# A causal attention layer in a hand-written order: follow-up pieces at set distances, the maximum subtracted on GpSimd, scores scheduled from the end

## The chip, the cores and the metric

The kernel runs on one core of one Trainium2 chip. A core has five engines that run side by side, each through its own instructions in a fixed order: TensorE (PE in the profile; its weight loads are PEld), VectorE (DVE), ScalarE (ACT), GpSimd (POOL) and SyncE (SP). Engines wait for one another through semaphores. The metric is the device time of one execution in microseconds (us); for a kernel with several runs it is their median.

## The reference

The input is an image of 256 channels and 64 x 64 pixels. Layer 0 is windowed linear attention over the image; the change does not touch it. Layer 1, which the change rewrites in part, treats the pixels as N = 4096 tokens of D = 256 numbers:

```python
t = t + attention(layer_norm(t))          # one head, causal, 4096 x 4096 scores
    A   = where(causal, q @ k.T, -32767) / 16;  out = softmax(A) @ v + x
    out = layer_norm(out) * g + b;  h = relu(out @ W1 + b1) @ W2 + b2
    result = layer_norm(h) * g + b
t = t + experts(layer_norm(t))
    logits = mean over all tokens of x @ Wr + br;  rw = softmax(logits)
    loads  = rw * 4096;  scale = where(loads > 640, 640 / loads, 1)
    rw = softmax(rw * scale);  the best two of 8 experts, for all tokens the same
    two-layer gelu networks of these two, weighted, and a layer_norm
```

The masked scores are filled with a finite number, so that the mask's own exponentials are also added up (`rest` and `after` below). All arithmetic is float32.

## The kernel before, in words

The whole kernel is one program of three stages. Layer 0 runs until about 978 us of the profile, the causal layer from there to about 1665 us, the router (which picks the two experts) to about 1681 us, and the experts to the end at 1908.8 us.

**The causal layer** works on 16 units `h`, each of 256 queries (two tiles of 128 tokens), and on key blocks `b` of 256 keys; unit `h` meets the blocks `h, h-1, ..., 0`. That makes 136 pairs `(h, b)`, in the order of the list `PAIRS`, where long and short units alternate. For each pair there are these steps:

- `scores(h, b)`: 4 matmuls on PE (8 records in the profile, since a float32 matmul shows as two) into the PSUM tile `pa`, L1051. ACT copies the scores to SBUF, `s<-pa`, L1063. DVE then updates a running elementwise maximum `max<-max,pa`, L1067. After the last block of a unit, DVE folds its two halves, L1070. The diagonal block goes through GpSimd for its mask, L1054 to L1060.
- `maxima(h)`: two pieces per unit. `over_keys` transposes the folded maximum on PE, L1080, and DVE reduces it, L1082 and L1086. `turn` transposes it back, L1093, and ACT copies it out as `tops`, L1095.
- `exponentials(h, b)`: DVE subtracts `tops` from the scores, L1102, and ACT takes the exponential, L1103. For the diagonal block the same is done for `rest`, L1106 and L1107.
- `products(h, b, j)`: for each of the two tiles `j`, 2 matmuls of the exponentials with the values into `po`, L1124 (and one of `rest`, L1127, on the diagonal). GpSimd normalises the residual `xn`, L1116, in a tile of which there is one.
- `finish(h, j)`: DVE divides by the softmax's sum and adds the residual, L1137 to L1139, then takes the statistics of the row.

When four tiles (a group `g`) are done, `layers(g, ...)` gives a list of 14 pieces that finish layer 1 for them: `root` (ACT's square root, which needs another activation table than the exponential: a table load of 1.28 us each way), `first` (DVE normalises, GpSimd adds a bias to `t`, L1172), `turn` (PE transposes, L1179; ACT copies, L1180), `hidden` twice (PE L1188, ACT L1190), `last` for each tile (PE L1197, DVE L1199), `root`, `scale` for each tile (DVE, L1207 and L1208), `root`, `norm` (DVE, L1216) and `turn_again` (PE transposes, L1224; ACT copies to `x2` and adds up each row, L1225).

**What sets the order.** PE, DVE and ACT run the instructions in the order in which the program issues them (`manual_schedule`); GpSimd's order is the scheduler's. The main loop runs over the 136 pairs: `score()` issues the scores of the pair that is 19 ahead (the ring of score tiles `s` has 20), `one()` issues one waiting piece, `raise_to(at + 2)` issues the exponentials up to two pairs ahead, then both `products`, then `one()` again. `one()` takes the oldest piece of the list `soon` (maxima, queries, mask fills), and if there is none the oldest of `later` (the layers' pieces). A piece is issued as soon as its turn comes, whether what it needs is ready or not; an engine that meets such an instruction waits. The last unit is walked tile by tile, `j = 1` and then `j = 0`, with all its exponentials issued before.

**The router**, `experts`, begins with the sum of `x2` over all tokens (L1334 to L1339), then a chain of small DVE and ACT operations that ends with the numbers of the two experts, four indirect DMAs from GpSimd's queue that fetch their weights (L1381), and small matmuls for the biases (L1394 to L1404). The experts' matmuls are L1418 and L1438.

Of the kernel before, what the change touches and what calls it, by code (L numbers as in the profile page):

```python
# [11 lines left out]
F32 = mybir.dt.float32  # L12
# [746 lines left out]
RING = 20  # L759
AHEAD = RING - 1  # L760


# [152 lines left out]
class Given:  # L915
# [3 lines left out]
    def __init__(self, nc, a, pool, causal):  # L919
# [21 lines left out]
        self.stats = tile("stats2", [P, NT, 2])  # L941
        self.sums = tile("sums2", [P, DC, NQ + 2])
        self.parts = 0


def causal_attention(tc, t, ident, eps5, causal, big, given):
# [7 lines left out]
    with ExitStack() as ctx:  # L954
# [33 lines left out]
        def behind():  # L988

            sums = sm.tile([NT, D + 1], F32, name="behind", bufs=1)  # L990
            later = sm.tile([NT, NT], F32, name="laters", bufs=1)
# [23 lines left out]
        def fills(h):  # L1015
# [22 lines left out]

            soon.append(turn)

# [58 lines left out]
        def exponentials(h, b):  # L1099
            u = units[h]  # L1100
            s = u[b].rearrange("p (k q) -> p k q", q=2 * P)
            nc.vector.tensor_tensor(s, s, u["top"].unsqueeze(1).to_broadcast([P, 2, 2 * P]), op=ALU.subtract)  # L1102
            nc.scalar.activation(u[b], u[b], AF.Exp, scale=1.0 / 16.0)  # L1103
            if b == h:
                rest = u["rest"].rearrange("p j q -> p (j q)")
                nc.vector.tensor_sub(rest, rest, u["top"][0:NT])  # L1106
                nc.scalar.activation(rest, rest, AF.Exp, scale=1.0 / 16.0)  # L1107
# [23 lines left out]
        def finish(h, j, acc):  # L1131
            i, g, xn = 2 * h + j, h // 2, units[h]["xn"]
            if g not in atts:
                atts[g] = (sm.tile([P, 4, D], F32, name="att"), sm.tile([P, 4, 2], F32, name="mvs", bufs=3), [])
            att, mvs, done = atts[g]
            l = sm.tile([P, 1], F32, name="l")
            nc.vector.reciprocal(l, acc[:, 0:1])  # L1137
            aj = att[:, i - 4 * g, :]
            nc.vector.scalar_tensor_tensor(aj, acc[:, 1:], l, xn[:, j, :], op0=ALU.mult, op1=ALU.add)  # L1139
            statistics(nc, sm, aj, mvs[:, i - 4 * g, :])  # L1140
            done.append(i)
            if 4 * g != BIG:
                if len(done) == 4:
                    later.extend(layers(g, 0, 4))
            elif len(done) == 2:
                later.extend(layers(g, 2, 4))
            elif len(done) > 2:
                new = layers(g, 4 - len(done), 5 - len(done))
                old = later[:]
                later.clear()  # L1150
                while new or old:
                    later.extend(new[:1] + old[:1])
                    del new[:1], old[:1]

        def layers(g, j0, j1):

            att, mvs, _ = atts[g]
            js, width = range(j0, j1), (j1 - j0) * P
            state = {}
# [53 lines left out]
            def norm():  # L1213
                inverse(mine)
                for j in js:
                    nc.vector.tensor_scalar(att[:, j, :].rearrange("p (c q) -> p c q", c=DC),  # L1216
                                            t[:, 4 * g + j, :].rearrange("p (q c) -> p c q", c=DC),
                                            mine[:, j, 0:1], mine[:, j, 1:2], op0=ALU.subtract, op1=ALU.mult)

            def turn_again():  # L1220
                for c in range(DC):
                    pt = psum()
                    for j in js:
                        nc.tensor.transpose(pt[:, (j - j0) * P : (j - j0 + 1) * P], att[:, j, c * P : (c + 1) * P], ident)  # L1224
                    nc.scalar.activation(x2[g][c][:, j0 * P : j1 * P], pt[:, 0:width], AF.Identity,  # L1225
                                         accum_out=given.sums[:, c, given.parts : given.parts + 1])
                given.parts += 1

            return ([lambda: root(mvs), first, turn] + [lambda e=e: hidden(e) for e in range(DC)]
                    + [lambda j=j: last(j) for j in js] + [lambda: root(state["mvy"])]  # L1230
                    + [lambda j=j: scale(j) for j in js] + [lambda: root(mine), norm, turn_again])

        soon, later = [], []

        def one():
            if soon:
                soon.pop(0)()
            elif later:
                later.pop(0)()

        E = mybir.EngineType
        with tc.manual_schedule(engines={E.PE, E.DVE, E.Activation}):
            blocks = [(h, b) for h in PAIRS for b in reversed(range(h + 1))]
            scored, raised = [0], [0]

            def queried(g):
                if g not in qTs:
                    soon.extend(queries(g))

            def score():  # L1250

                at = scored[0]
                if at == len(blocks):
                    return
                scored[0] += 1
                h, b = blocks[at]
                if b == h:
                    while "rest" not in units[h] or not qTs[h // 2][1]:
                        soon.pop(0)()
                    n = PAIRS.index(h) + 1  # L1260
                    if n < len(PAIRS):
                        fills(PAIRS[n])
                        queried(PAIRS[n] // 2)
                scores(h, b)
                if b == 0:
                    soon.extend([lambda: None] + maxima(h))

            def raise_to(at):
                while raised[0] < min(at + 1, len(blocks)):
                    h, b = blocks[raised[0]]  # L1270
                    while "top" not in units[h]:
                        soon.pop(0)()
                    exponentials(h, b)
                    raised[0] += 1
# [4 lines left out]
            causal.values(7, psum)  # L1279
            soon.extend(behind())  # L1280
            fills(PAIRS[0])
            for at in range(AHEAD):
                score()
                one()
                if at in (0, 6):
                    causal.values(6 - at // 6, psum)
                if at == PAIRS[0] + 1:
                    causal.values(4, psum)
            raise_to(1)
            done = [len(blocks) - 1 - PAIRS[-1]]  # L1290
            for at, (h, b) in enumerate(blocks[: done[0]]):
                score()
                one()
                raise_to(at + 2)
                for j in range(2):
                    products(h, b, j)
                one()
            h = PAIRS[-1]
            raise_to(len(blocks))
            for j in (1, 0):  # L1300
                for b in reversed(range(h + 1)):
                    products(h, b, j)
                    for _ in range(2 - j):
                        one()
            while soon or later:
                one()
        return x2


def experts(tc, a, t, out, ident, eps5, given, x2):  # L1310
# [4 lines left out]
    with ExitStack() as ctx:  # L1315
# [16 lines left out]

        xsum = w.tile([P, DC], F32, name="xsum")
        nc.vector.tensor_reduce(xsum, given.sums, AX.X, ALU.add)  # L1334
        every = w.tile([P, DC, P], F32, name="every")
        nc.vector.tensor_copy(every, xsum.unsqueeze(2).to_broadcast([P, DC, P]))
        pl = ps.tile([P, 512], F32, name="pr", bufs=1)
        for c in range(DC):
            nc.tensor.matmul(pl[:, 0:NE], lhsT=every[:, c, :], rhs=given.wr[:, c, :], start=(c == 0), stop=(c == DC - 1))  # L1339
        x = cols("rx")  # L1340
# [3 lines left out]
        sc = cols("sc")  # L1344
        nc.vector.tensor_scalar(sc, rw, float(N), 1.0, op0=ALU.mult, op1=ALU.max)
        nc.vector.reciprocal(sc, sc)
        nc.vector.tensor_scalar(sc, sc, CAPACITY, 1.0, op0=ALU.mult, op1=ALU.min)
        nc.vector.tensor_mul(sc, sc, rw)
        rw = softmax(sc, "sb")
# [15 lines left out]
        hot = w.tile([P, 3, NE], F32, name="hot")  # L1365
        tmp = cols("tmp")
        w1 = w.tile([P, 2, DC * FF], F32, name="w1")
        w2 = w.tile([P, 2, FC * D], F32, name="w2")
        views = [(w1, a["W1e"].rearrange("(r c) f -> r (c f)", c=DC)), (w2, a["W2e"].rearrange("(r c) d -> r (c d)", c=FC))]
        ixs = []  # L1370
        for e in range(2):
            nc.vector.tensor_scalar(hot[:, e, :], rank, float(e), None, op0=ALU.is_equal)
            nc.vector.tensor_mul(tmp, hot[:, e, :], given.ei)
            at = cols(f"at{e}", 1)
            nc.vector.tensor_reduce(at, tmp, AX.X, ALU.add)
            ix = w.tile([P, 1], I32, name=f"ix{e}")
            nc.vector.scalar_tensor_tensor(ix, at, float(P), given.pi, op0=ALU.mult, op1=ALU.add)
            ixs.append(ix)
        for dst, src in views:
            for e in range(2):  # L1380
                nc.gpsimd.indirect_dma_start(  # L1381
                    out=dst[:, e, :], out_offset=None, in_=src,
                    in_offset=bass.IndirectOffsetOnAxis(ap=ixs[e][:, 0:1], axis=0),
                )
        two = cols("two", 2)
        for e in range(2):
            nc.vector.tensor_mul(tmp, hot[:, e, :], rw)
            nc.vector.tensor_reduce(two[:, e : e + 1], tmp, AX.X, ALU.add)
        tw = softmax(two, "sc2")
# [94 lines left out]
```

## Time and profile before

| what | value |
|---|---|
| runs shown | 1910.74, 1914.86, 1917.91 us; median 1914.86 us |
| the profiled execution's own time | 1910.61 us |
| its span, first to last instruction | 1908.8 us |
| mean granted TensorE clock | 0.979 |
| PE / DVE / ACT / POOL busy over the span | 95% / 53% / 43% / 27% |
| causal layer, PE's last product | 978 to 1652.5 us |
| end of layer 1's pieces, first use of their sum by PE | 1666.4 us |
| first experts' matmul, and their unbroken run | 1678.4 us, 1681.6 us |

How to read it: every group of instructions is named by its line, its engine, and the tiles that it writes and reads. "Idle before" is the time in which the engine stood still just before an instruction, and the arrow names what ended that. PE's busy time contains matmuls that run at half the clock, so the granted clock has to be read with it.

### The profile page before, as it was taken

What the parts mean: (1) busy time and instruction counts of PE and PEld (TensorE: products, weight loads), DVE (VectorE), ACT (ScalarE), POOL (GpSimd) and SP (SyncE); (2) the same over time, 40 slices, a digit from 0 to 9 for tenths busy, and PEclk for the clock granted to TensorE, in tenths of its full rate; (3) what the DMA queues carried; (4) which work ended last, traced back from release to release, by engine and by line L of the source; (5) the groups of instructions that cost most, each with busy time, mean ns of one, the idle gap of its engine ahead of it and who ended that gap; (6) DMA issues with size and microseconds to landing.
All of it is one profiled execution on the core that took longest, in us unless ns stands there. A gap on an engine that the chain in (4) does not pass through costs nothing.

```text
span 1908.8 us, 50513 instructions
## 1 busy us (share of the span) xinstructions
PE 1811.1 (95%) x22336; PEld 1323.6 (69%) x22336; DVE 1012.5 (53%) x2019; ACT 828.6 (43%) x1498; POOL 510.0 (27%) x761
## 2 busy tenths in 40 slices
PE   6999999999999999999999999999999888689998
PEld 4666667666666667766678786776777676468777
DVE  7534666655644577667644346445554555533343
ACT  3566444444456644445313335444444434322332
POOL 2493233430254134432120202202112110122120
PEclk9999999999999999999999999999999899789999
DMA  5321100000421100002000000000000000010000
GB/s 177 109 92 63 31 19 16 18 14 20 131 74 36 47 21 18 14 14 53 13 2 1 0 1 1 1 1 1 1 1 1 1 1 1 0 56 11 22 23 22
DMA packets 66651, 53.61 MB, mean 28 GB/s; under 512 B 37312, under 2 KB 56536, under 8 KB 66432
## 3 DMA queue, kind: packets, MB, share of 16 engines
q1 hardware_dynamic: 52688, 27.67, 5.3%
q10 hardware_dynamic: 12480, 18.87, 2.9%
q0 software_dynamic: 1264, 3.84, 0.7%
q8 instruction: 175, 2.87, 0.6%
q14 instruction: 44, 0.36, 0.1%
HBM read 32.93 MB, written 17.44 MB: 26 GB/s over the span
## 4 chain that ended last, share of the span: by engine, by line
PE 42%; DVE 8%; ACT 3%; issue 1%; POOL 0%; ACTq 0%; DVEq 0%
PE pa L1051 10%; PE po L1124 8%; PE ph L1418 6%; PE py L1438 6%; PE pm L1188 2%; PE pm L980 1%; PE pm L1197 1%; DVE max L1067 1%; PE acc L405 1%; DVE lnst L747 1%; PE ps L372 1%; DVE s L1102 1%; ACT s L1063 1%; PE pm L910 1%; PE ps L519 1%
## 5 line engine op out<-in xcount | busy, mean ns | idle before, releaser
L340 ACT ACTIVATE pm<-ps 128x512 f32<-128x512 f32 (+24 forms) x690 | 358.4, 584 | 344.1 <-issue 188.0
L342 DVE TENSOR_SCALAR pm<-ps 128x512 f32<-128x512 f32 (+21 forms) x414 | 265.4, 669 | 264.4 <-PE ps L372 178.2
L372 PE MATMUL ps<-q,kh 32*128 32x217 f32 (+27 forms) x3872 | 212.1, 336 | 0.0
L405 PE MATMUL acc<-pm,vh 128*32 128x217 f32 (+27 forms) x3872 | 199.7, 329 | 0.0
L1051 PE MATMUL pa<-qT,k 128*128 128x256 f32 (+1 forms) x800 | 191.2, 385 | 0.0
L1067 DVE TENSOR_TENSOR max<-max,pa 128x512 f32<-128x512 f32 x105 | 71.8, 684 | 213.7 <-ACT s L1063 213.6
L1051 PEld LDWEIGHTS pa<-qT,k 128*128 128x128 f32 x800 | 153.6, 196 | 24.5 <-issue 3.3
L372 PEld LDWEIGHTS ps<-q,kh 32*128 32x128 f32 x3872 | 160.6, 185 | 9.8
L1103 ACT ACTIVATE s<-s 128x512 f32<-128x512 f32 x136 | 85.5, 630 | 166.7 <-DVE s L1102 166.6
L440 POOL TENSOR_TENSOR y<-y,rn 128x512 f32<-128x512 f32 x32 | 41.0, 1282 | 410.1 <-DVE y L439 410.1
L405 PEld LDWEIGHTS acc<-pm,vh 128*32 128x32 f32 x3872 | 98.0, 109 | 71.8 <-issue 37.1
L363 PE MATMUL ps<-table,table 32*128 32x184 bf16 (+37 forms) x2904 | 141.2, 246 | 5.0 <-ACT pm L340 1.8
L363 PEld LDWEIGHTS <-table 32*128 32x128 bf16 x2904 | 57.6, 92 | 108.0 <-issue 96.1
L1063 ACT COPY s<-pa 128x512 f32<-128x512 f32 x120 | 69.8, 581 | 128.8 <-PE pa L1051 128.5
L1438 PE MATMUL py<-w,hT 128*128 128x256 f32 x512 | 111.8, 379 | 0.0
L1438 PEld LDWEIGHTS py<-w,hT 128*128 128x128 f32 x512 | 97.3, 190 | 15.7 <-issue 1.9
L372 PE MATMUL ps<-q,k 32*128 32x192 f32 (+30 forms) x1936 | 104.1, 338 | 0.5 <-issue 0.5
L1124 PE MATMUL po<-kh,s 128*128 128x257 f32 x406 | 102.6, 385 | 0.9 <-ACT s L1103 0.9
L405 PE MATMUL acc<-pm,v 128*32 128x192 f32 (+30 forms) x1936 | 96.1, 326 | 0.9 <-issue 0.9
L1116 POOL TENSOR_SCALAR xn<-t,stats 128x256 f32<-128x256 f32 x32 | 41.7, 1309 | 205.9 <-DVE att L1139 196.2
L1102 DVE TENSOR_TENSOR s<-s,tops 128x512 f32<-128x512 f32 x136 | 94.3, 698 | 0.0
L519 PE MATMUL ps<-l0wo,y 128*128 128x256 f32 x384 | 90.7, 387 | 0.0
(318 smaller groups left out, 2987.0 us busy)
## 6 DMA issues: line engine op xcount, KB each, us to landing
oscratch<-ov ACTq DMA_DIRECT2D x32, 256.0 KB
ov<-oscratch SPq DMA_DIRECT2D x32, 256.0 KB
vscratch<-v SPq DMA_DIRECT2D x32, 128.0 KB
vh<-vscratch SPq DMA_DIRECT2D x16, 256.0 KB
t<-in_xT ACTq DMA_DIRECT2D x16, 256.0 KB
raw<-in_x SPq DMA_DIRECT2D x7, 512.0 KB
raw<-in_x ACTq DMA_DIRECT2D x7, 512.0 KB
out<-y SPq DMA_DIRECT2D x7, 512.0 KB
```

Of the source, the lines that this page charges most:

```text
L340: nc.scalar.activation(dst, src, AF.Relu)
L342: nc.vector.tensor_scalar_max(dst, src, 0.0)
L363: nc.tensor.matmul(got[h][:, spot].rearrange("p (y x) -> p y x", y=part.r1 - part.r0), lhsT=spread[hs, int(part.vertical), :], rhs=bias[hs ...
L372: nc.tensor.matmul(got[h][:, spot].rearrange("p (y x) -> p y x", y=part.r1 - part.r0), lhsT=keys[hs], rhs=q[hs, part.r0 : part.r1, part.c0 ...
L405: nc.tensor.matmul(out, lhsT=v, rhs=pm[:, h, spot].rearrange("p (y x) -> p y x", y=part.r1 - part.r0), start=fresh, stop=(left[key] == 0), ...
L519: nc.tensor.matmul(pt[:, i * D : (i + 1) * D], lhsT=ys[wi, Y][:, (2 * j + i) * P : (2 * j + i + 1) * P], rhs=wo[:, n, :], start=(n == 0), ...
L1051: nc.tensor.matmul(pp[:, k * 2 * P + at : (k + 1) * 2 * P], lhsT=key, rhs=qT[:, c, q0 + at : q0 + 2 * P], start=(c == 0), stop=(c == DC - 1))
L1067: nc.vector.tensor_tensor(u["max"], old, pp, op=ALU.max)
L1102: nc.vector.tensor_tensor(s, s, u["top"].unsqueeze(1).to_broadcast([P, 2, 2 * P]), op=ALU.subtract)
L1124: nc.tensor.matmul(acc, lhsT=u[b][:, (2 * k + j) * P : (2 * k + j + 1) * P], rhs=v[2 * b + k][:, 0 : D + 1], start=(b == h and k == 0), st ...
L1418: nc.tensor.matmul(ph, lhsT=w1v[:, e, c, f, :], rhs=x2[g][c], start=(c == 0), stop=(c == DC - 1))
L1438: nc.tensor.matmul(py, lhsT=hT[:, e, f, j * P : (j + 1) * P], rhs=w2v[:, e, f, :], start=(e + f == 0), stop=(e == 1 and f == FC - 1))
```

## The change

It leaves layer 0 and the experts' loops as they are. In the causal layer:

- Each waiting piece has a distance now. A counter `now` goes up by 2 after each `score()` and by 1 after each tile's `products`. A piece is due when `now` has gone up by its distance since the piece before it in its list.
- Each group of layers' pieces is a `Line` of its own. While scores are left, the oldest line with a due piece gives one, and the next comes at the earliest 2 later. A third line cannot start before the oldest is emptied. Once all scores are issued, the due line with the most pieces left gives one.
- The subtraction of the maximum goes from DVE to GpSimd, for all 136 pairs and for `rest`, and GpSimd's instructions also run in the order of the program.
- Exponentials are issued three pairs ahead instead of two; in the last unit they are issued along its walk.
- A score is issued at the latest place from which its unit's maximum is still complete `LEAD = 4` pairs before it is used, instead of always 19 ahead.
- The last tile's part of the sum over tokens comes from a matmul with a column of ones before its `turn_again`; the other parts are added up beforehand. The router's `scale` becomes one minimum, and its operations for the two experts are done for both at once.

```diff
@@ Causal layer
-            soon.append(turn)
+            soon.steps.append((1, turn))
...
-            nc.vector.tensor_tensor(s, s, u["top"].unsqueeze(1).to_broadcast([P, 2, 2 * P]), op=ALU.subtract)
+            nc.gpsimd.tensor_tensor(s, s, u["top"].unsqueeze(1).to_broadcast([P, 2, 2 * P]), op=ALU.subtract)
...
-                nc.vector.tensor_sub(rest, rest, u["top"][0:NT])
+                nc.gpsimd.tensor_sub(rest, rest, u["top"][0:NT])
...
             if g not in atts:
+                while len(later) > 1:
+                    later[0].take()
...
-                    later.extend(layers(g, 0, 4))
+                    later.append(Line(layers(g, 0, 4)))
...
+            def total():
+                pt = psum()
+                for c in range(DC):
+                    nc.tensor.matmul(pt[:, c : c + 1], lhsT=att[:, j0, c * P : (c + 1) * P], rhs=causal.bvc[:, 0:1],
+                                     start=True, stop=True)
+                nc.vector.tensor_tensor(given.every, pt[:, 0:DC].unsqueeze(2).to_broadcast([P, DC, P]),
+                                        given.others.unsqueeze(2).to_broadcast([P, DC, P]), op=ALU.add)
...
+            far = 3 if j1 - j0 == 4 else 2
+            return [(2, lambda: root(mvs)), (far, first), (far, turn), (2, lambda: hidden(0)), (1, lambda: hidden(1)),
+                    *((2, lambda j=j: last(j)) for j in js), (2, lambda: root(state["mvy"])),
+                    *((far if j == j0 else 2, lambda j=j: scale(j)) for j in js), (2, lambda: root(mine)), (far, norm),
+                    *[(1, total)] * final, (far, turn_again)]
+
+        class Line:
+            def __init__(self, steps=()):
+                self.steps, self.last = list(steps), now[0]
+            def due(self):
+                return self.steps and now[0] >= self.last + self.steps[0][0]
...
-        def one():
-            if soon:
-                soon.pop(0)()
-            elif later:
-                later.pop(0)()
+        def one(n):
+            now[0] += n
+            if soon.due():
+                soon.take()
+            elif now[0] >= spaced[0]:
+                due = [line for line in later if line.due()]
+                if due and scored[0] < len(blocks):
+                    due[0].take()
+                    spaced[0] = now[0] + 2
+                elif due:
+                    max(due, key=lambda line: len(line.steps)).take()
 
         E = mybir.EngineType
-        with tc.manual_schedule(engines={E.PE, E.DVE, E.Activation}):
+        with tc.manual_schedule(engines={E.PE, E.DVE, E.Activation, E.Pool}):
...
                 scores(h, b)
                 if b == 0:
-                    soon.extend([lambda: None] + maxima(h))
+                    soon.steps.extend(zip((2, 2), maxima(h)))
+                    soon.last = now[0]
...
-            raise_to(1)
-            done = [len(blocks) - 1 - PAIRS[-1]]
-            for at, (h, b) in enumerate(blocks[: done[0]]):
-                score()
-                one()
-                raise_to(at + 2)
+            latest, first = [], [at for at, (h, b) in enumerate(blocks) if b == h]
+            for at in reversed(range(len(blocks))):
+                h, b = blocks[at]
+                latest.append(min(first[PAIRS.index(h)] - LEAD - b, latest[-1] - 1 if latest else len(blocks)))
+            latest.reverse()
+            raise_to(2)
+            end = len(blocks) - 1 - PAIRS[-1]
+            for at, (h, b) in enumerate(blocks[:end]):
+                if scored[0] < len(blocks) and latest[scored[0]] <= at:
+                    score()
+                    one(2)
+                raise_to(at + 3)
                 for j in range(2):
                     products(h, b, j)
-                one()
+                    one(1)
+
             h = PAIRS[-1]
-            raise_to(len(blocks))
             for j in (1, 0):
-                for b in reversed(range(h + 1)):
+                for at, b in enumerate(reversed(range(h + 1))):
+                    raise_to(end + at + 3)
                     products(h, b, j)
-                    for _ in range(2 - j):
-                        one()
-            while soon or later:
-                one()
+                    one(1)
+                    one(0)
+            while later:
+                for line in list(later):
+                    line.take()
@@ router
-        nc.vector.tensor_scalar(sc, rw, float(N), 1.0, op0=ALU.mult, op1=ALU.max)
-        nc.vector.reciprocal(sc, sc)
-        nc.vector.tensor_scalar(sc, sc, CAPACITY, 1.0, op0=ALU.mult, op1=ALU.min)
-        nc.vector.tensor_mul(sc, sc, rw)
+        nc.vector.tensor_scalar_min(sc, rw, CAPACITY / N)
...
-        for e in range(2):
-            nc.vector.tensor_scalar(hot[:, e, :], rank, float(e), None, op0=ALU.is_equal)
-            nc.vector.tensor_mul(tmp, hot[:, e, :], given.ei)
+        nc.vector.tensor_tensor(hot[:, 0:2, :], both(rank), given.ei[:, 0:2].unsqueeze(2).to_broadcast([P, 2, NE]),
+                                op=ALU.is_equal)
+        nc.vector.tensor_mul(tmp, hot[:, 0:2, :], both(given.ei))
...
```

## The prediction

> **What bounds the kernel now.** I read the engines' busy shares first (PE 95%), then PE's waits in the causal layer, then the stretches of that layer with the granted clock, and then single stalls on the timeline. PE is the bound throughout, so only what it waits for, what runs at half the clock, and the serial ends of the stage can be won. PE's waits from 978 to 1652.6 us (columns: total, times, longest):
>
> ```profile
> PE pm L1224 <- DVE att L1216: 19.0, 6, 5.2
> PE pm L1080 <- DVE fold L1070: 10.3, 13, 4.1
> PE pm L1179 <- DVE att L1171: 9.0, 11, 3.8
> PE pm L1093 <- DVE wide L1086: 4.6, 4, 2.1
> PE pm L1188 <- ACT aT L1180: 1.6, 1, 1.6
> ```
>
> With three shorter rows (0.9, 0.3, 0.3) that is 46.0 us. Nearly all of it is a transpose that was issued too soon after the DVE work that feeds it. The second cost is the clock, in the eighth number of the rows by stage:
>
> ```profile
> 1020.00:1185.00 165.00, 162.76 (x721) 129.84 (x720) 75.10 (x155) 64.29 (x114) 27.37 (x46) 1.00 0.00 1
> 1185.00:1585.00 400.00, 368.55 (x1581) 289.29 (x1580) 204.09 (x471) 174.87 (x303) 60.12 (x100) 0.96 0.00 1
> 1585.00:1652.60 67.60, 55.47 (x220) 40.20 (x218) 36.47 (x100) 27.38 (x46) 9.34 (x8) 0.92 0.00 0
> ```
>
> A clock of 0.96 over 400 us and of 0.92 over 67.6 us is at most 16.0 + 5.4 = 21.4 us of lost PE work; part of it falls into waits, so I take 17. While it is low, a group of 8 products takes 3.20 us (at 1190.27) instead of 1.74 (at 1051.29). The low stretches last about 3.4 us, some 1.7 us lost each, so there are about ten.
>
> **Part 1, layers' pieces at set distances.** Before, `one()` issues a piece per half pair, ready or not. L1224, L1179, L1188 and L1197 wait 19.0 + 9.0 + 1.6 + 0.3 = 29.9 us. In the changed order at least 1.73 us of scores or products lie between two pieces, and three such units between `root` and `first` and between `norm` and `turn_again`. What these chains need is known: the jam at 1418 to 1423 is L1102 0.66, exponential 0.63, table load 1.28, root 0.30, and four L1216 in 1.39 us, which three units (5.2 us) cover up to a few tenths. I leave 3 us of waits, which gives **27**. The extra table loads' place on ACT does not change their number.
>
> **Part 2, the second maximum piece (turn, L1093).** It stands 1.74 to 2.6 us of PE work behind the first now. Its chain is a DVE reduction and a 256-wide maximum, about 1.2 us by their rows: 4.6 us of waits go to 0.3, **4.3** won.
>
> **Part 3, the first maximum piece (over_keys).** This is the part that costs. Before, a unit's last scores, then one tile pair's products, then the transposes L1080. The timeline of one such unit:
>
> ```profile
> 1576.88 1.89 PE L1051 MATMUL pa<-qT,k 128*128 128x256 f32 x8
> 1578.61 1.90 PE L1124 MATMUL po<-vh,s 128*128 128x257 f32 x8
> 1578.87 0.58 ACT L1063 COPY s<-pa 128x512 f32<-128x512 f32 x1 [0.89 <-PE pa L1051]
> 1579.48 0.69 DVE L1067 TENSOR_TENSOR max<-max,pa 128x512 f32<-128x512 f32 x1 [2.17 <-ACT s L1063]
> 1580.21 0.42 DVE L1070 TENSOR_TENSOR fold<-max 128x256 f32<-128x256 f32 x1
> 1580.69 0.44 PE L1080 MATMUL pm<-ident,fold 128*128 128x128 f32 x2 [0.18 <-DVE fold L1070]
> ```
>
> From the products' start at 1578.61 (PE's last score step) to the transposes at 1580.69 are 2.08 us: copy, maximum, fold. The products cover 1.74 of it, and 0.34 is left as a stall. In the changed order `soon.last` is set when the last scores are issued, and `one(2)` follows at once: the distance of 2 is already met. In 14 of the 16 units the transposes come right behind the scores, with no PE work between. PE runs in order, so all 2.08 us are a wait, and the products queue behind it. 14 x 2.08 = 29.1, plus 1.4 for the slower DVE beside GpSimd, is 30.5 against 10.3: **-20.2**. The two other units have 1.96 and 3.91 us between and cost nothing more.
>
> **Part 4, the clock.** The long waits of parts 1 and 2 (1.8 to 5.4 us) go, and with them their half-clock stretches. The new ones are of 2.08 us with 0.44 us of transposes behind them. Three places say what such a wait does:
>
> ```profile
> 1188.32 1.95 PE L1224 MATMUL pm<-ident,att 128*128 128x128 f32 x8 [1.76 <-DVE att L1216]
> 1190.00:1194.00 4.00, 4.00 (x14) 3.25 (x13) 1.29 (x2) 3.40 (x8) 0.00 (x0) 0.61 0.02 4
> ...
> 1292.38 0.44 PE L1093 MATMUL pm<-ident,wide 128*128 128x128 f32 x2 [2.15 <-DVE wide L1086]
> 1288.00:1294.00 6.00, 3.68 (x19) 2.41 (x18) 4.68 (x13) 2.07 (x5) 3.27 (x5) 1.00 0.00 0
> ```
>
> A wait of 1.76 us with 8 transposes behind it was followed by a clock of 0.61, one of 2.15 us with two transposes was not (1.00), nor were those of 1308 to 1310 us. As if transposes counted as rest, and the clock fell when a fixed stretch of 3.4 us is under about 0.3 busy: 2.08 + 0.44 = 2.52 us can do that (2.4 needed), but only when it lies inside one stretch, about one time in three. So 4 of 14, at 1.7 us: 7 of the 17 stay, **10** won. The bounds are 0 and 14 x 1.7 = 24. The Trainium skill, "TensorE: Matmul & The Clock Gate", Part 1, has the clock go back to half after at least one idle window of about 3.4 us; by it none of these waits would do it and the 7 would be 0; but by it the wait of 1.76 us above wouldn't either, and its row shows 0.61.
>
> **Part 5, the subtraction on GpSimd.** Nearest rows: a two-input GpSimd operation of this size, and the subtraction on DVE now.
>
> ```profile
> L440 POOL TENSOR_TENSOR y<-y,rn 128x512 f32<-128x512 f32 x32 | 41.0, 1282 | 410.1 <-DVE y L439 410.1
> L1102 DVE TENSOR_TENSOR s<-s,tops 128x512 f32<-128x512 f32 x136 | 94.3, 698 | 0.0
> ```
>
> I take 1.28 us (bounds 1.08, from L559 with one operand twice, and 2.62, twice the 1.31 of the half-size `xn`, L1116). 136 x 1.28 = 174 us on top of about 100 that GpSimd has in this stage, out of 674: not a bound, and not at 2.62 either (456). PE needs about 3.47 us per pair, so each subtraction hides; what DVE gets free (94 us) is the reason why parts 1 and 2 can keep their distances and isn't counted again. What shows is order, for GpSimd now runs in program order and a waiting instruction holds up all subtractions behind it. At the start, the `diag` and `rest` selections of unit 0 wait for ACT's fill ahead of the first subtraction: 2 to 2.5 us. Once `xn` (2.6 us for two tiles) and the wide fills stand ahead of the subtractions of a new unit: about 2. In the tail, the last unit's exponentials come behind `xn` and the bias adds of the layer (0.7 each): 2.0 + 1.7. Together **-8**. Bounds: nothing, since three pairs ahead (10.4 us) cover xn + subtraction + exponential (4.5 us); and 16 x 1.9 = 31, if each unit's first subtraction comes late by the whole 2.62 - 0.70. The Trainium skill, "GPSIMD Engine Reference", 4.1 Engine selection, sends elementwise work on tiles to VectorE, GpSimd being about twice as slow for two inputs. The rows agree (1282 to 698); on the path it would be 136 x 0.58 = 79 us slower, off the path nothing, and PE's 3.47 us per pair say that it is off.
>
> **Part 6, scores late, and the end.** The number of matmuls is the same; scores run to place 125 of 129 instead of 117, so about 3.5 us of layer work on PE moves behind the last product, which comes 3.5 earlier. But the last tile's `first` then has 5.8 us of DVE work of other lines ahead of it (norm of four tiles 1.55, two scales 3.2, `last` and statistics 1.0), of which 4.6 adds to the end: **-1.1**.
>
> **Part 7, sum over tokens and router.** Four small DVE operations (0.85) become one (0.2): 0.65. The index operations go from 1.93 to 1.17: 0.75. The sum by a matmul takes some 0.3 off the chain, the order of the bias matmuls 0.2. All lie on the serial chain from 1666 to 1678 us: **1.9**. The table load before it and the indirect DMAs (4.6 us from issue to landing) stay, only start earlier.
>
> **Sum:** 27 + 4.3 - 20.2 + 10 - 8 - 1.1 + 1.9 = 13.9. The profiled execution took 1910.6 (span 1908.8), so 1896.7 on its scale. It lies 4.2 us under the runs' median, 1914.9; I add half of that and forecast **1898.7**.
>
> **Rivals** (all with the same 2 us added).
> - *The maxima's waits take over and halve the clock: slower.* DVE's two-input operations slow down while GpSimd runs (L1207 0.45 to 0.81 at 1558.98), and GpSimd is now busy over a third of the time. At a factor of 1.7, maximum and fold take 0.78 more, the wait is 2.86, with the transposes 3.3 of a 3.4 us stretch, and each one gates: 14 x 0.78 = 11, and 24 - 7 = 17 more at half clock: +28, **1926.6**. It decides when the wait with its transposes exceeds 2.4 us in any position. For it: 1188.32. Against: 1292.38, and that most folds would miss a subtraction.
> - *Everything hides.* No new wait gates (7), GpSimd is never late (8), the end's DVE work fits into waits (4.6): 19.6 less, **1879.1**. For it: 1292.38 and the 10.4 us of lead. Against: the order itself at start and tail.
> - *GpSimd's order makes exponentials late in each unit.* `xn` is one tile, so its instruction waits for the unit before to finish and holds the subtractions: 16 x 0.75 = 12 more, **1910.7**, no change. Against: three pairs of lead; for: a single queue with `xn`, fills and bias adds in it.
> - *The change does not do what it says* has little room: the distances stand in the issued order.
>
> **Numbers.** Forecast 0.44, everything hides 0.24, GpSimd late 0.19, slower 0.13. The range goes from just under the second rival to between the third and the first, 1876 to 1922, which also takes in the bounds of the clock (-7, +17) and most of GpSimd's 31. 0.5% (9.6 us) is about what a measurement here can tell from no change. Faster by more needs under 1905.3: the second rival and most of the forecast, 0.60; within: the third and the rest, 0.27; slower: 0.13.
>
> **What would show it.** In the changed profile: waits of the over_keys transposes for DVE's fold at about 30 us over 14 or 15; those of the layers' transposes under 4; a clock of about 0.985 between 1185 and 1585; 136 GpSimd subtractions at about 1.28 us; PE waiting for ACT's exponentials at the start and in the tail, about 8 in all; 1.5 to 2 us less from the last layer piece to the first experts' matmul. I am wrong if the over_keys waits are much shorter (then copy, maximum and fold overlap with something) or PE waits for exponentials throughout.

## The result and the profile after

The changed kernel's median is 1909.39 us (1896.67 to 1912.28), the kernel before 1916.01 us in the same comparison; the ratio is 0.9962, 95% interval 0.9939 to 0.9986. So it is faster by 0.4%, where 0.85% was forecast: the right sign, a little under half the size. The profiled execution has a span of 1907.7 us, 1.1 us less than before, and a mean clock of 0.981.

PE's waits in the changed kernel, from 978 us to its last product at 1645.5 us (total, times, longest):

```profile
PE pm L1082 <- DVE fold L1072: 31.8, 15, 5.8
PE pm L1178 <- DVE att L1170: 7.8, 6, 4.1
PE po L1126 <- ACT s L1105: 6.1, 3, 2.7
PE pm L1029 <- POOL wide L1023: 1.6, 2, 1.0
PE po L1126 <- DVE att L1143: 1.6, 1, 1.6
PE pm L1232 <- DVE att L1215: 0.9, 1, 0.9
```

L1082, L1178, L1232 and L1126 are what L1080, L1179, L1224 and L1124 were. The waits add up to 49.8 us, against 46.0: they moved from the layers' pieces (29.9 to 8.7) to the maximum's transposes (10.3 to 31.8). The clock hardly moved either. It is the number behind the five engines' busy times in the rows by stage: 0.97 from 978 us to the last product in both kernels, and 0.96 between 1185 and 1585 us in both, where the prediction wanted to see about 0.985:

```profile
978.00:1645.50 667.50, 617.53 (x2693) 491.84 (x2694) 260.87 (x584) 263.98 (x468) 281.32 (x324) 0.97 0.00 1
1185.00:1585.00 400.00, 367.32 (x1596) 291.46 (x1595) 170.24 (x389) 167.28 (x295) 158.02 (x186) 0.96 0.00 1
```

One of the new waits on the timeline:

```profile
1071.78 1.89 PE L1053 MATMUL pa<-qT,k 128*128 128x256 f32 x8
1073.76 0.58 ACT L1065 COPY s<-pa 128x512 f32<-128x512 f32 x1 [2.34 <-PE pa L1053]
...
1074.38 0.69 DVE L1069 TENSOR_TENSOR max<-max,pa 128x512 f32<-128x512 f32 x1 [2.77 <-ACT s L1065]
1075.10 0.43 DVE L1072 TENSOR_TENSOR fold<-max 128x256 f32<-128x256 f32 x1
1075.58 0.44 PE L1082 MATMUL pm<-ident,fold 128*128 128x128 f32 x2 [1.91 <-DVE fold L1072]
```

It is the chain of the prediction, copy, maximum and fold, with no products beside it. Thirteen of the 15 waits are of this kind, 1.85 to 2.27 us each and 25.2 us together; one is 0.75 us. The longest, 5.81 us, has another cause:

```profile
1399.24 1.28 ACT L1161 ACT_TABLE_LOAD   x1
...
1403.87 0.30 ACT L1161 ACTIVATE stats<-stats,eps 128x4 f32<-128x4 f32 x1 [3.35 <-DVE stats L748]
1404.18 1.28 ACT L1105 ACT_TABLE_LOAD   x1
...
1406.01 0.57 ACT L1065 COPY s<-pa 128x512 f32<-128x512 f32 x1
...
1407.81 0.48 PE L1082 MATMUL pm<-ident,fold 128*128 128x128 f32 x1 [5.81 <-DVE fold L1072]
```

PE's last scores end at 1402.0 us, but their copy starts 4.0 us later. In ACT's queue it stands behind a `root` of the layers' pieces, which had loaded its table and then stood 3.35 us waiting for VectorE's statistics.

To see where the time went, I add up a ledger: each step from the start of one matmul record to the next is split into its length at full clock (work; 0.22 us for a 256-wide record), as much again where it started at half clock, what is left over if that is more than 0.3 us (waits), and what is left over if it is less (rest). From 978 us to the last product, in us:

| execution | work | half clock | waits | rest | sum |
|---|---|---|---|---|---|
| before | 584.1 | 18.3 | 52.4 | 18.2 | 673.0 |
| changed | 582.0 | 16.1 | 54.3 | 13.7 | 666.1 |
| changed, a second execution (below) | 582.0 | 7.4 | 53.9 | 14.1 | 657.4 |

From the last product to the first matmul that uses the sum over tokens it is 14.0 us before and 19.4 after, from there to the experts' PE work 12.0 and 12.2. So 6.9 us were won in the loop, 5.4 given back behind it and 0.2 in the router: 1.3 us.

### The profile page after: what moved, and what is told of

The parts are those of the page before. It is cut to its first block, busy times and chain, and to the rows that moved or that the text cites. A ratio compares the mean times of both kernels' runs of the same rounds, so it can differ in the third digit from the quotient of the medians.

```text
span 1907.7 us, 50488 instructions
## 1 busy us (share of the span) xinstructions
PE 1806.2 (95%) x22340; PEld 1325.4 (69%) x22340; DVE 944.6 (50%) x1858; ACT 818.2 (43%) x1490; POOL 686.0 (36%) x913
## 4 chain that ended last, share of the span: by engine, by line
PE 45%; DVE 5%; POOL 1%; ACT 1%; issue 1%; ACTq 0%; DVEq 0%; POOLq 0%
PE po L1126 11%; PE pa L1053 10%; PE ph L1457 6%; PE py L1477 6%; PE pm L1187 2%; PE pm L1196 1%; PE pm L982 1%; PE acc L405 1%; PE ps L372 1%; DVE max L1069 1%; DVE att L1170 1%; PE pm L911 1%; PE po L1129 1%; PE ps L519 1%; ACT s L1065 1%
## 5 line engine op out<-in xcount | busy, mean ns | idle before, releaser
L1104 POOL TENSOR_TENSOR s<-s,tops 128x512 f32<-128x512 f32 x136 | 170.4, 1277 | 204.8 <-ACT tops L1097 204.8
L1053 PE MATMUL pa<-qT,k 128*128 128x256 f32 (+1 forms) x800 | 185.7, 377 | 0.0
L1126 PE MATMUL po<-kh,s 128*128 128x257 f32 x406 | 106.6, 392 | 3.3 <-ACT s L1105 3.3
L1126 PE MATMUL po<-v,s 128*128 128x257 f32 x342 | 90.5, 397 | 4.3 <-ACT s L1105 2.7
```

The source lines that it names most:

```text
L1053: nc.tensor.matmul(pp[:, k * 2 * P + at : (k + 1) * 2 * P], lhsT=key, rhs=qT[:, c, q0 + at : q0 + 2 * P], start=(c == 0), stop=(c == DC - 1))
L1104: nc.gpsimd.tensor_tensor(s, s, u["top"].unsqueeze(1).to_broadcast([P, 2, 2 * P]), op=ALU.subtract)
L1126: nc.tensor.matmul(acc, lhsT=u[b][:, (2 * k + j) * P : (2 * k + j + 1) * P], rhs=v[2 * b + k][:, 0 : D + 1], start=(b == h and k == 0), st ...
```

## Experiments

**The theory** from these rows: the maximum's waits and the half clock behind them ate the gain. **Rivals**: VectorE, slowed beside GpSimd's subtractions, is what is late; or the router's and the end's chains.

**The same kernel again** (no edit):

> The changed kernel once more, to set the later versions against it on the same chip. If the first result stands, 0.994 to 0.9985 of the kernel before; if the chip of the first result was a matter of chance, within 0.2% of it.

Ratio 0.9958 (0.9934 to 0.9981): the result stands. What differs is the profiled execution, with a span of 1898.2 us. Its waits for the maximum are the same:

```profile
PE pm L1082 <- DVE fold L1072: 31.5, 15, 5.8
```

But the time at half clock in the loop is 20.5 us instead of 41.0 (44.4 before), by the clock record. The same wait near 1074 us has a clock of 0.91 around it in the first execution and 1.00 in the second:

```profile
1060.00:1080.00 20.00, 18.09 (x79) 15.26 (x78) 4.71 (x8) 5.87 (x11) 0.18 (x1) 0.91 0.00 0
```

```profile
1060.00:1080.00 20.00, 18.03 (x88) 15.42 (x87) 4.03 (x7) 6.46 (x14) 2.73 (x5) 1.00 0.00 0
```

One program, one wait (1.91 and 1.92 us), two outcomes: its length does not settle whether it halves the clock. In each execution the half-clock stretches lie on a grid of 3.41 us, and the two grids are shifted against each other by 2.6 us, so that a wait falls elsewhere on it. That is the likely reason, but it isn't shown to be the whole one. In the first execution the waits of 1.91 us that end at 1376.3 and at 1436.8 lie each inside one stretch, with PE busy for 1.50 us of it, and only the first is followed by half the clock:

```profile
1373.41:1376.82 3.41, 1.50 (x9) 1.02 (x8) 1.52 (x5) 1.11 (x2) 0.00 (x0) 1.00 0.00 0
1376.82:1380.23 3.41, 3.41 (x10) 2.67 (x9) 1.08 (x3) 0.00 (x0) 0.00 (x0) 0.50 0.00 0
1434.85:1438.26 3.41, 1.50 (x9) 1.35 (x9) 1.96 (x4) 1.41 (x3) 0.00 (x0) 1.00 0.01 2
1438.26:1441.68 3.42, 3.42 (x22) 3.05 (x21) 0.00 (x0) 1.19 (x4) 0.41 (x1) 1.00 0.00 0
```

The kernel's ten runs fit such a draw: the fastest (1896.67 us) had a mean clock of 0.987, the slowest (1912.28) of 0.979.

**The first maximum piece later** (products between the last scores and the transposes):

```diff
-                    soon.last = now[0]
+                    soon.last = now[0] + 2
```

> The changed kernel with one tile pair's products put back between a unit's last scores and the transposes for its maximum. Theory (the transposes' wait and the half clock behind it ate the gain): of the 31.8 us that PE waits there about 28 go, and about 8 of 12 half-clock stretches of 1.7 us with them, 13 us; 1909 becomes 1868 to 1880. Rival (VectorE, slowed beside GpSimd, is what is late): the waits move to the next piece and less than 10 us are won, 1900 to 1909.

1892.15 us, 0.9901 (0.9873 to 0.9929): 0.6 points better than the change, between the two expectations. Half of the wait was only passed on, to the second piece, which now has one group of scores ahead of it:

```profile
PE pm L1095 <- DVE wide L1088: 13.6, 11, 2.9
PE pm L1178 <- DVE att L1170: 7.5, 6, 3.9
PE po L1126 <- ACT s L1105: 6.8, 3, 3.5
PE pm L1082 <- DVE fold L1072: 4.6, 9, 2.4
```

**The wait filled with redundant matmuls** (the transposes overwrite what they give):

```diff
                 pt = psum()
+                for k in range(4):
+                    nc.tensor.matmul(pt[:, 0 : 2 * P], lhsT=x[0][k % DC][:, 0:P], rhs=x[0][k % DC][:, 0 : 2 * P],
+                                     start=True, stop=True)
```

> The changed kernel with four redundant matmuls (about 1.74 us on PE, overwritten at once) ahead of each unit's maximum transposes, so that PE works instead of waiting; the output is unchanged. Theory that these waits halve the clock: the half-clock stretches behind them go (8 of 12, 13 us) while the wait itself is only filled: 1894 to 1900. Rival (the clock is not set by these waits, only by the long ones): no gain, 1907 to 1914.

1898.28 us, 0.9938 (0.9918 to 0.9959). PE does 28 us more (610.5 us of work in the ledger) and the kernel is not slower. By the medians' ratios it is 0.2% faster than the change, but the intervals overlap. Half clock in the loop is 13.7 us by the clock record, the lowest with the maxima at their place. The direction is that of the theory; the size expected, 10 to 15 us, is not shown, since the change itself loses 7 to 16 us there, as it falls.

**The maxima at once in the kernel before** (the empty piece ahead of them taken out):

```diff
-                    soon.extend([lambda: None] + maxima(h))
+                    soon.extend(maxima(h))
```

> The kernel before with one thing changed: the transposes for a unit's maximum follow its last scores at once, with no products between. Theory: 16 waits grow by about 1.74 us each, 25 us with more half-clock stretches behind them: 1935 to 1950 against 1915. Rival (products that come later only fill another wait in this order): under 8 us, 1915 to 1923.

1936.45 us, 1.0122 (1.0089 to 1.0155), as the theory had it. The row of L1080:

```profile
PE pm L1080 <- DVE fold L1070: 35.3, 15, 5.0
```

That is 25.0 us over the 10.3 of before. Other waits shrink beside it: up to the last product all of them are 62.1 us, 16.1 more than before. The time at half clock grows as well, from 44.4 to 78.5 us, in an execution that was the slowest of its six runs (1943.03 us). This one distance costs 1.2%.

**The subtractions back on VectorE** (in the changed kernel):

```diff
-            nc.gpsimd.tensor_tensor(s, s, u["top"].unsqueeze(1).to_broadcast([P, 2, 2 * P]), op=ALU.subtract)
+            nc.vector.tensor_tensor(s, s, u["top"].unsqueeze(1).to_broadcast([P, 2, 2 * P]), op=ALU.subtract)
...
-                nc.gpsimd.tensor_sub(rest, rest, u["top"][0:NT])
+                nc.vector.tensor_sub(rest, rest, u["top"][0:NT])
```

> The changed kernel with both subtractions back on VectorE, all else kept. Theory that VectorE's operations are slowed by GpSimd's subtractions: the four normalising operations of the layer's first piece fall from 870 ns to about 350 in the mean, the waits of the layer's transposes (11 us with the tail) to about 3, the one maximum wait of 5.8 us to 2, ACT's late exponentials (6.1 us) to 2, and some four half-clock stretches go (7 us): 1888 to 1897. Rival (VectorE's own 94 us of subtractions cost the same in its queue): the maximum's waits grow by 0.7 us each, 1905 to 1920.

1907.69 us, 0.9981 (0.9960 to 1.0002): no gain, as the rival had it. The slowing was there, the time was not. The layer's normalising operation, first in the changed kernel and then here:

```profile
L1170 DVE TENSOR_SCALAR att<-att,mvs 128x256 f32<-128x256 f32 x32 | 26.1, 870 | 0.4
```

```profile
L1170 DVE TENSOR_SCALAR att<-att,mvs 128x256 f32<-128x256 f32 x32 | 11.7, 423 | 0.4
```

One case of the slowing in the changed kernel: four of these operations take 6.66 us, one of them alone 4.47, and it ends just behind the third of three subtractions on GpSimd:

```profile
1453.78 6.66 DVE L1170 TENSOR_SCALAR att<-att,mvs 128x256 f32<-128x256 f32 x4
...
1456.27 3.69 POOL L1104 TENSOR_TENSOR s<-s,tops 128x512 f32<-128x512 f32 x3
...
1460.16 0.80 PE L1178 MATMUL pm<-ident,att 128*128 128x128 f32 x2 [4.06 <-DVE att L1170]
```

With the subtractions on VectorE the waits at L1178 fall from 7.8 to 3.5 us, but the maximum's grow from 31.8 to 36.0, with VectorE's 93 us of subtractions in the same queue. A long one of 5.4 us, as at 1407.8, is still among them, so GpSimd's slowing is not what makes it.

**Only the subtractions moved, in the kernel before** (the same edit in the other direction; GpSimd's order is the scheduler's):

> The kernel before with nothing changed but the engine of the two subtractions, GpSimd in place of VectorE. Theory that VectorE's queue of subtractions made the layer's transposes late (29.9 us of waits): these waits fall by a third or more, 1895 to 1905. Rival (VectorE's operations beside GpSimd take twice as long, and the distance alone was what was missing): the layer's normalising operations go from 450 to about 850 ns, waits as before or longer, 1908 to 1925.

1955.85 us, 1.0230 (1.0200 to 1.0260): slower than either the theory or the rival said. On the timeline a fold of 0.43 us takes 17.51, while GpSimd goes from one subtraction to the next; the last run of six ends at 1088.17, the fold at 1088.45:

```profile
1070.94 17.51 DVE L1070 TENSOR_TENSOR fold<-s 128x256 f32<-128x256 f32 x1 [3.81 <-POOL s L1060]
...
1080.82 7.35 POOL L1102 TENSOR_TENSOR s<-s,tops 128x512 f32<-128x512 f32 x6
...
1088.60 0.66 PE L1080 MATMUL pm<-ident,fold 128*128 128x128 f32 x2 [15.86 <-DVE fold L1070]
```

**Both maximum pieces later**, with a pair between them:

```diff
-LEAD = 4
+LEAD = 5
...
-                    soon.steps.extend(zip((2, 2), maxima(h)))
-                    soon.last = now[0]
+                    soon.steps.extend(zip((2, 4), maxima(h)))
+                    soon.last = now[0] + 2
```

> The changed kernel with products between a unit's last scores and its first maximum transposes, and a whole pair between these and the second ones, made room for by LEAD = 5. Theory (these two waits and the half clock behind them ate the gain): with only the first moved, 13.6 us of waits stood at the second one; these go, and three or four half-clock stretches (6 us) with them: about 0.980 to 0.984 of the kernel before, 1872 to 1880. Rival (the scores come too early now and something else is late): no better than with the first alone, 0.990.

1870.26 us, 0.9785 (0.9755 to 0.9814), slightly better than the theory's range: it holds. `LEAD = 5`, which makes the room, has not been run alone. The largest waits left in the loop are these:

```profile
PE pm L1232 <- DVE att L1215: 7.1, 2, 6.8
PE pm L1178 <- DVE att L1170: 6.6, 5, 3.9
PE po L1126 <- ACT s L1105: 4.1, 3, 1.7
```

**The same with the subtractions on VectorE** (both edits above):

> The version with both maximum pieces later, with the subtractions back on VectorE. Theory that VectorE slowed beside GpSimd is now what is late: the waits of the layer's transposes fall from about 11 us to 6, the late exponentials of start and tail go down by 2: 4 to 10 us faster than the same on GpSimd, 0.976 to 0.981. Rival (GpSimd's relief is worth as much as its slowing costs): within 3 us of the same on GpSimd. Third: VectorE's queue with 94 us more makes the maxima late again: 5 us slower.

1859.19 us, 0.9731 (0.9702 to 0.9761), the fastest version: 2.7% under the kernel before, 0.55 points better than with GpSimd, and slightly better than the theory's range. Its largest waits in the loop:

```profile
PE po L1126 <- ACT s L1105: 4.4, 2, 2.6
PE pm L1178 <- DVE att L1170: 3.3, 2, 1.9
PE pm L1082 <- DVE fold L1072: 3.3, 8, 1.1
```

Its ledger is 579.8 work, 4.8 half clock, 19.1 waits, 11.9 rest.

**The same with redundant work on GpSimd:**

```diff
+            for _ in range(2):
+                nc.gpsimd.tensor_tensor(given.every, u["top"].rearrange("p (c q) -> p c q", c=DC),
+                                        u["top"].rearrange("p (c q) -> p c q", c=DC), op=ALU.subtract)
```

> Both maximum pieces later, subtractions on VectorE, and for each pair two redundant GpSimd subtractions of 128x256 (about 1.4 us together) into a tile that nobody reads until the sum over tokens overwrites it. Theory that a GpSimd two-input operation slows VectorE's operations on SBUF tiles beside it: the layer's normalising operations go from 420 to 800 ns or more, its waits rise, 0.977 to 0.984 of the kernel before instead of 0.973, as with the subtractions on GpSimd itself. Rival (it is the exponentials' dependence on GpSimd's queue that costs): 0.972 to 0.975.

1871.98 us, 0.9811 (0.9785 to 0.9836), though nothing reads what these operations write before the sum. A version without them (`m6` below) took 1859.84 us in the same comparison. The normalising operation (L1173 here) shows a reason:

```profile
L1173 DVE TENSOR_SCALAR att<-att,mvs 128x256 f32<-128x256 f32 x32 | 16.8, 580 | 0.4
```

It is 580 ns instead of 420, less than the 800 expected. The waits for exponentials are those of the fastest version, 4.6 against 4.4 us. So work on GpSimd that no exponential waits for costs about as much (12 us) as the subtractions there (11 us), and the exponentials' dependence on GpSimd isn't needed to explain the cost. The slowing of VectorE is the main suspect. The redundant operations also stand ahead of GpSimd's own residual and mask work in its queue, and no run separates the two; the wait that passes through the residual (products behind L1146) is 2.7 us here and 1.9 in the fastest version.

**The layers' pieces at distance 1** (in the fastest version; the spacing of 2 between any two stays):

```diff
-            far = 3 if j1 - j0 == 4 else 2
-            return [(2, lambda: root(mvs)), (far, first), (far, turn), (2, lambda: hidden(0)), (1, lambda: hidden(1)),
+            far = 1
+            return [(1, lambda: root(mvs)), (far, first), (far, turn), (1, lambda: hidden(0)), (1, lambda: hidden(1)),
...
```

> Both maximum pieces later, subtractions on VectorE, but the layers' pieces at distance 1, so that only the spacing of 2 between any two keeps them apart (3 from root to first, to the transposes and from norm to turn_again before). Theory that the distances remove the layers' waits: these come back to 10 to 25 us, 0.978 to 0.988 of the kernel before. Rival (moving the maxima and the scores made room, the distances do little): 0.973 to 0.976.

1871.81 us, 0.9811 (0.9786 to 0.9836): the distances are worth 0.7 to 0.8 points, 12 to 15 us, by `m6` in the same comparison and by the fastest version. Up to the last product the transposes at L1232 wait 7.3 us for VectorE again, against 0.3. Those at L1178 do not: 1.6 us, against 3.3. All waits in the ledger are 28.9 us against 19.1.

**GpSimd's order left to the scheduler** (`m6`; in the fastest version, `E.Pool` taken from the list of engines):

> Both maximum pieces later, subtractions on VectorE, and GpSimd's order left to the scheduler again. Theory that GpSimd's program order costs time at the start and in the tail: PE's waits for exponentials (4.4 us) and for the layer's bias and residual work fall by 2 to 4 us, 0.971 of the kernel before. Rival (without the subtractions GpSimd has nothing in its queue that holds up anyone): within 0.15% of 0.973.

1859.84 us, 0.9741 (0.9717 to 0.9765): the rival holds, within 0.15%; the waits for exponentials stay at 4.4 us.

**The router alone**, in the kernel before (the diff's minimum and its operations for two experts):

> The kernel before with only the router's shorter operations (one minimum in place of four, the numbers of the two experts at once). By the prediction's step 1.4 us less between the router's first result and the experts' first matmul, 0.9993 of the kernel before. Rival, by the trace of the changed kernel (VectorE fills what is saved with other work that the scheduler puts in the chain, and DMAs start no earlier): 0 to 0.3 us.

1913.87 us, 1.0014 (0.9992 to 1.0035), too small to time. In the trace it is 9.84 us from the first result (1665.18) to the bias matmul that now opens the experts' PE work (1675.02), against 10.98 before: 1.1 us won. In the changed kernel the same stretch is 11.11. VectorE's rows there, from the first result on:

```profile
1666.06 0.17 DVE L1385 SCALAR_TENSOR_TENSOR rx<-pr,br 128x8 f32<-128x8 f32 x1 [0.47 <-PE pr L1383]
1666.14 0.68 DVE L740 TENSOR_SCALAR xn<-t,stats 128x256 f32<-128x256 f32 x1
1666.74 0.15 DVE L1374 TENSOR_REDUCE sam<-rx 128x1 f32<-128x8 f32 x1
1666.82 1.04 DVE L740 TENSOR_SCALAR xn<-t,stats 128x256 f32<-128x256 f32 x2
1667.78 0.15 DVE L1377 RECIPROCAL sas<-sas 128x1 f32<-128x1 f32 x1
1667.97 0.41 DVE L1378 TENSOR_SCALAR sae<-sae,sas 128x8 f32<-128x8 f32 x1
1668.41 0.56 DVE L1389 TENSOR_SCALAR sc<-sae 128x8 f32<-128x8 f32 x1
```

The scheduler put the experts' residual (L740) between the links of the chain. From the first result to the operation of the minimum (L1389) it is 2.35 us here and 1.48 with the router's edit alone.

No run takes by itself the 5.4 us at the end, the exponentials three pairs ahead, or the sum over tokens by a matmul.

## Why the prediction was right in sign and twice too large

Two steps of the prediction failed. Part 1 took VectorE's durations as known, and Part 4 set one number for what is a draw. Parts 6 and 7 were mis-sized by about 2 us each.

- **Part 1 (27): 21.2 measured, a step that failed by a wrong reason.** "What these chains need is known" took VectorE's durations from the kernel before. Beside GpSimd's operations the normalising operation takes up to 4.5 us instead of 0.41, and L1178 waits 7.8 us, where under 4 was expected for all the layers' transposes; with the subtractions back on VectorE it is 3.5. The rival "the maxima's waits take over" had the slowing, a factor of 1.7, but put it on the maximum, which reads PSUM and stayed at 0.68 us.
- **Part 4, the clock (10): 2.2 measured, mis-sized, the largest miss.** The prediction had "4 of 14" waits halve the clock for one stretch each, so that 7 of 17 us would stay. In the profiled execution six of the maximum's waits did, three of them for two stretches, and the ledger keeps 16.1 of 18.3 us. In the second execution it was two waits, and 10.9 us were won; that this is nearly the forecast is a draw too. A range was due where the text set one number.
- **Part 3, the maxima (-20.2): right in its chain, lucky in its sum.** 31.8 us over 15 waits against 30.5 over 14; the loss is 21.5. But the waits of its kind are shorter than it said, 1.94 us in the mean and not 2.08, and the total is made up by the one wait of 5.81 us behind ACT's `root`, of which the prediction said only that the number of table loads stays. Undoing this one distance, and the second that it passes the wait on to, takes the change from 0.996 to 0.9785.
- **Part 2 (4.3): right** in the change, where no wait at L1095 is left. It comes back as 13.6 us as soon as only the first piece moves.
- **Part 5 (-8): right in sum**, 9.3 us of waits for exponentials, mask rows and the like, 8.4 more than before. But it looked at GpSimd's queue alone and had nothing for what GpSimd's work does to VectorE.
- **Part 6 (-1.1): -3.3 measured.** Work worth 2.1 us moved behind the last product, not 3.5, and the end took 5.4 longer, not 4.6. Why it did was not tested.
- **Part 7 (1.9): -0.2 measured**, though the same edit of the router in the kernel before wins 1.1. The saved operations were counted, but not what a scheduler puts in the gap.

By the ledger, waits as a whole were to fall by 3.1 us and grew by 1.9. With the clock (7.8 short in the profiled execution), the end (2.2) and the router (2.1) that is 17.1 us, more than the 12.6 that are missing between the two profiled executions (13.9 forecast, 1.3 in the ledger). The ledger's rest goes the other way by 4.5 us, which the prediction did not have and whose cause is open.

Of the rivals, "everything hides" falls with the waits themselves. "GpSimd late" gave nearly the time, 1910.7, for another reason: exponentials are late in three places in the loop, not in each unit.

## What to carry to other kernels

When an order is written out by hand, give every transpose that waits for a chain its own distance from the last link, and check the distance at the place of issue: a counter that is set before its own increment made a distance of 2 into none, and the same distance taken out of the kernel before cost 1.2%. Before work is moved to an idle engine, price what it does to the neighbour that it slows, not only to the queue that it joins. Where a piece stands in ScalarE's queue ahead of such a chain, ask what that piece waits for. And where a wait may halve the clock, forecast a range: two executions of one program differed by 9 us in it.

## What the runs showed of the hardware

- VectorE beside GpSimd's operations, in the changed kernel: the layers' elementwise operations that read only SBUF slow down (`first`, L1170, from 407 ns alone to 1465 with over half their time beside GpSimd's; `scale`, L1206, from 464 to 845; `norm`, L1215, from 408 to 637; means), while those that read PSUM (maximum 684 and 682, L1198 420 and 418, L1143 484 and 483) and the row statistics (427 and 428) do not change at all. The Trainium skill, "SBUF — State Buffer", section "SBUF: two separate sides", speaks of an exclusive lock of a port pair that these two engines share, held for the whole instruction, the other fully blocked. The rows agree with the block. They show more than one instruction of it, though: 17.51 us lasted through a dozen subtractions.
- A wait of 1.9 us can halve the clock or not, from one execution to the next. The Trainium skill, "TensorE: Matmul & The Clock Gate", Part 1, calls the window that the clock is judged by free-running, which fits the shifted grids; that a window must be wholly idle does not, as the stretch from 1373.41 us shows, with PE busy for 1.50 of its 3.41 us and a clock of 0.50 behind it.
- Left open: why a run of GpSimd operations sometimes lets VectorE in after one of them and sometimes after twelve, and whether anything in a program can set the phase of the clock's stretches.
